# A four-layer graph network on one core: steps of the edge gathers, and the transposing loads, put at other pieces of a strip

## The chip, the cores and the metric

The kernel runs on one core of a Trainium2 chip. The metric is the device time of one execution in microseconds; the number compared is the median of several runs. The engines are named as in the profile: PE (matrix products), PEld (its weight loads), DVE (vector), ACT (scalar), POOL (GpSimd) and SP (sync, here a pure DMA issuer). A gather on POOL is an indirect DMA: POOL makes its descriptors, the DMA engines move the data afterwards.

## The reference, cut to what matters

6,250 nodes with 128 features pass through four pre-normalised graph layers over the same 206,250 edges, which are sorted by destination. All four need sums over edges; the first weights them:

```
msg = edge_val[:, None] * x[edge_src]
neighbor = jax.ops.segment_sum(msg, edge_dst, num_segments=N_NODES)
...
agg = jax.ops.segment_sum(x[src], dst, num_segments=n)          # layers 1 and 3
summed = jax.ops.segment_sum(gathered, node_idx, num_segments=n_nodes)   # layer 2: the other way round
```

Each is a product with a node-by-node matrix that holds how many edges (or what sum of weights) run between two nodes. The kernel builds that matrix once and uses it as a dense one.

## The kernel before, in words

**Two stages.** The first (here the *build*, from the start to about 1120 us in the trace) makes the matrix of counts and, on the way, layer 0. The second (`dense`, L890) multiplies by the stored counts for layers 1 to 3. The change touches the build alone.

**Strips and pieces.** The build walks 25 strips (`strip`, L825) of 256 destination nodes; the last has one block of 128, 106 of them real. A strip is cut into 32 counts of four windows each, and eight pieces, numbered 0 to 7, of four counts. For one count (`count`, L722) PE makes 24 pairs of weight load and product from two one-hot tiles, `s_hot` (source within its block of 128) and `k_hot` (number of the block, also times the three parts of the weight), into a PSUM tile `pK` of which there are three; then ACT copies it twice (L741): to `cnt` (counts) and `edge_w` (weights). DVE makes the one-hots of a piece a piece ahead (`one_hots`, L703, three instructions at L715, L717 and L718; two buffers each, so the ones for piece n+2 can start when PE is through with piece n). When half a strip is counted, that is after pieces 3 and 7, SP stores the block `cnt` to memory (L843, 1568 KB).

**What is threaded between the pieces.** After each piece the strip advances several generators by one step, in this order (L846 to L857):
- `end`: the end of layer 0 for the strip before last (`finish0`, L774), at pieces 0 to 5 and 7. Its step at piece 0 loads `xs0`, that at piece 4 stores two blocks (L799, L800), that at piece 7 one (L815).
- `edges`: the edges of the next strip (`prepare`, L628), at pieces 1, 3, 5 and 6. Its steps are: find by a comparison (L633 to L638) where the strip's edges start, and gather `line`; refine that (L643 to L663) and gather the first half of `dst`; count the matches (L669, L671), and gather the second half of `dst` and then `src` and the weights, each in two halves (five gathers, all issued by L625); after that turn them to keys (L676 to L688, DVE and POOL); transpose them on PE and copy them on ACT (L692, L697). The first of these steps, for the strip after next, is taken at piece 7.
- `before`: one eighth of layer 0's product for the strip before (`layer0`, L760): 12 or 14 products of `h0` and `edge_w`, at every piece.
- `turns` (`turn`, L743): one load that transposes seven blocks of counts (L751) and the store of the transposed load before it (L753), 175 of each in all, one at every piece from strip 1 on.

**What sets the order.** Strips 1 to 23 are under a manual schedule, so each engine runs its instructions in the order in which the program writes them; a step of a generator that waits holds up all that stands behind it on its engine. Strips 0 and 24 are ordered by the scheduler. POOL holds, in a strip: `line`, `dst`, `dst`, `src`, weights, `src`, weights, one addition of `finish0` (L798) and four instructions of `split` (L574 to L577). SP holds the stores of counts, the loads and stores of `turn` and those of `finish0`.

Of the kernel before, what the change touches and what calls it, by code (L numbers as in the profile page):

```python
# [469 lines left out]
NS = len(STRIPS)  # L470
# [16 lines left out]
def fast(ctx: ExitStack, tc: tile.TileContext, a: dict, out: bass.AP, flag: bass.AP):  # L487
# [84 lines left out]
    def split(eng, parts, src, rest):  # L572

        eng.tensor_copy(parts[0], src)  # L574
        eng.tensor_tensor(rest, src, parts[0], op=ALU.subtract)
        eng.tensor_copy(parts[1], rest)
        eng.tensor_tensor(parts[2], rest, parts[1], op=ALU.subtract)  # L577
# [7 lines left out]
    with ExitStack() as bx:  # L585
# [38 lines left out]
        def fetch(t, name, idx):  # L624
            nc.gpsimd.indirect_dma_start(out=t, out_offset=None, in_=col[name],  # L625
                                         in_offset=bass.IndirectOffsetOnAxis(ap=idx, axis=0))

        def prepare(k):  # L628

            n0 = node0[:, k : k + 1]  # L630
            junk = once.tile([P, NSMP], BF16, name="junk")
            r = small.tile([P, 1], F32, name="r")
            nc.vector.tensor_scalar(junk, smp, n0, None, op0=ALU.is_lt, op1=ALU.add, accum_out=r)  # L633
            at = small.tile([P, 1], F32, name="at")
            nc.vector.tensor_scalar(at, r, 1.0, 0.0, op0=ALU.subtract, op1=ALU.max)
            nc.vector.tensor_scalar(at, at, float(P), float(E - P), op0=ALU.mult, op1=ALU.min)
            at_i = small.tile([P, 1], I32, name="at_i")
            nc.vector.tensor_copy(at_i, at)  # L638
            line = once.tile([P, P], I32, name="line")
            fetch(line, "dst", at_i)  # L640
            yield
            less = once.tile([P, P], BF16, name="less")
            nc.vector.tensor_scalar(less, line, n0, None, op0=ALU.is_lt)  # L643
            c = small.tile([P, 1], F32, name="c")
            nc.vector.tensor_reduce(c, less, axis=mybir.AxisListType.X, op=ALU.add)
            off = small.tile([P, 1], F32, name="off")
            nc.vector.tensor_add(off, at, c)

            dst = once.tile([P, P], I32, name="dst")
            src = once.tile([P, P], I32, name="src")  # L650
            wgt = once.tile([P, P], F32, name="wgt")
            vals = pay.tile([P, 5, P], BF16, name="vals")
            same = once.tile([P, P], BF16, name="same")
            other = once.tile([P, P], BF16, name="other")
            halves_of = [(h, slice(h * H, (h + 1) * H)) for h in range(WN)]
            offs, nodes = [], []
            for h, half in halves_of:
                off_i = small.tile([P, 1], I32, name="off_i")
                nc.vector.tensor_scalar(off_i, off, float(E - H), None, op0=ALU.min)  # L659
                fetch(dst[:, half], "dst", off_i)  # L660
                offs.append(off_i)
                node = small.tile([P, 1], F32, name="node")
                nc.vector.tensor_scalar(node, n0, float(h), None, op0=ALU.add)  # L663
                nodes.append(node)
                if h + 1 == WN:
                    break
                yield
                here = deg[:, k, h : h + 1]
                nc.vector.tensor_scalar(same[:, half], dst[:, half], node, None, op0=ALU.is_equal,  # L669
                                        op1=ALU.add, accum_out=here)  # L670
                nc.vector.tensor_add(off, off, here)  # L671
            for (h, half), off_i in zip(halves_of, offs):
                fetch(src[:, half], "src", off_i)
                fetch(wgt[:, half], "edge_weight", off_i)
            yield
            nc.vector.tensor_scalar(same[:, half], dst[:, half], node, None, op0=ALU.is_equal,  # L676
                                    op1=ALU.add, accum_out=deg[:, k, WN - 1 : WN])
            for (h, half), node in zip(halves_of, nodes):
                nc.vector.tensor_scalar(other[:, half], dst[:, half], node, float(2 * P),
                                        op0=ALU.not_equal, op1=ALU.mult)  # L680
            sb = once.tile([P, P], I32, name="sb")
            nc.vector.tensor_scalar(sb, src, 7, None, op0=ALU.arith_shift_right)
            nc.vector.tensor_tensor(vals[:, 1, :], other, sb, op=ALU.add)
            sl = once.tile([P, P], I32, name="sl")
            nc.vector.tensor_scalar(sl, src, P - 1, None, op0=ALU.bitwise_and)
            nc.vector.tensor_copy(vals[:, 0, :], sl)
            rest = once.tile([P, P], F32, name="rest")
            split(nc.gpsimd, [vals[:, i, :] for i in (2, 3, 4)], wgt, rest)  # L688
            yield
            pv = psum.tile([P, 5, P], BF16, name="pD")  # L690
            for i in range(5):
                nc.tensor.transpose(pv[:, i, :], vals[:, i, :], identh)  # L692
            keys = pay.tile([P, P // TI, 2, TI], BF16, name="keys")
            parts = pay.tile([P, P // TI, 3, TI], BF16, name="by_edge")
            for t, i in ((keys, 0), (parts, 2)):
                to = pv[:, i : i + t.shape[2], :].rearrange("p i (q t) -> p q i t", t=TI)
                nc.scalar.copy(t, to)  # L697
            by_edge = keys, parts
            yield by_edge
# [3 lines left out]
        def one_hots(by_edge, t0):  # L703

            of = slice(t0 // TI, t0 // TI + tq)
            keys, parts = (t[:, of, :, None, :] for t in by_edge)

            def at(i, n):
                return keys[:, :, i].to_broadcast([P, tq, n, TI])

            def count_up(n):
                return iota[:, None, :n, :].to_broadcast([P, tq, n, TI])

            s_hot = hot.tile([P, tq, P, TI], BF16, name="s_hot")
            nc.vector.tensor_tensor(s_hot, count_up(P), at(0, P), op=ALU.is_equal)  # L715
            k_hot = hot.tile([P, tq, 4, NB, TI], BF16, name="k_hot")
            nc.vector.tensor_tensor(k_hot[:, :, 0], count_up(NB), at(1, NB), op=ALU.is_equal)  # L717
            nc.vector.tensor_tensor(k_hot[:, :, 1:], k_hot[:, :, :1].to_broadcast([P, tq, 3, NB, TI]),  # L718
                                    parts.to_broadcast([P, tq, 3, NB, TI]), op=ALU.mult)
            return s_hot, k_hot  # L720
# [101 lines left out]
        edges = prepare(1)  # L822
        next(edges)

        def strip(k, nb):  # L825
            nonlocal before, edges, by_edge, hots
            edge_w = edge.tile([P, NB, SW], F32, name="edge_w")
            end = ends.pop() if ends else iter(())
            last, piece, following = nb * P // WN, 0, None
            for w0 in range(0, last, PW):  # L830
                if w0 % TW == 0:
                    now, t1 = hots, w0 + TW
                    if t1 < last:
                        hots = one_hots(by_edge, t1)
                    elif following:
                        hots = one_hots(following, 0)
                if w0 * WN % P == 0:
                    cnt = cnts.tile([P, NB, P], BF16, name="cnt")
                count(w0, now, cnt, edge_w)
                g, w1 = k * SB + w0 * WN // P, w0 + PW  # L840
                if w1 * WN % P == 0:
                    c, i = CHUNK_OF[g]
                    nc.sync.dma_start(cnt_d[c, :, i, :], flat(cnt))  # L843
                if w1 % (PW * PT) and w1 < last:
                    continue
                if piece != 6:  # L846
                    next(end, None)
                if piece in (1, 3, 5):
                    next(edges, None)
                elif piece == 6:  # L850
                    following = next(edges, None)
                next(before, None)
                if piece == 7 and k + 2 < NS:
                    edges = prepare(k + 2)
                    next(edges)
                if k and piece < 8:
                    next(turns, None)  # L857
                piece += 1
            by_edge = following
            for _ in chain(before, end):  # L860
                pass
            before = layer0(k, nb, edge_w)
# [327 lines left out]
```

## Time and profile before

| | |
|---|---|
| median of 3 runs | 2080.66 us (2076.43 to 2086.75) |
| profiled execution | 2135.14 us |
| its span in the trace | 2133.1 us |
| mean granted clock of PE | 0.969 |
| busy over the span: PE, PEld, DVE, ACT, POOL | 1905.6, 1551.1, 1392.8, 1176.7, 403.6 us |
| ACT copies of `pK` (L741), two kinds, 784 of each | 404.5 and 413.1 us |
| gathers (L625), `dst` alone, 50 | 82.4 us, 1648 ns each |

Busy time counts when an engine has an instruction of its own in work. The share of the whole span says little here, since the build and the dense stage have different limits; what follows reads the build alone. "Idle before, and what ended it" names the last semaphore that came before an instruction could start; "remote" stands for a semaphore that rose at a moment where the profile has no instruction's end to go with it, "issue" for no wait that the profile shows.

### The profile page before, as it was taken

What the parts mean: (1) busy time and instruction counts of PE and PEld (TensorE: products, weight loads), DVE (VectorE), ACT (ScalarE), POOL (GpSimd) and SP (SyncE); (2) the same over time, 40 slices, a digit from 0 to 9 for tenths busy, and PEclk for the clock granted to TensorE, in tenths of its full rate; (3) what the DMA queues carried; (4) which work ended last, traced back from release to release, by engine and by line L of the source; (5) the groups of instructions that cost most, each with busy time, mean ns of one, the idle gap of its engine ahead of it and who ended that gap; (6) DMA issues with size and microseconds to landing.
All of it is one profiled execution on the core that took longest, in us unless ns stands there. A gap on an engine that the chain in (4) does not pass through costs nothing. (4 is left out here: it accounts for less than half of the span.)

```text
span 2133.1 us, 60004 instructions
## 1 busy us (share of the span) xinstructions
PE 1905.6 (89%) x25624; PEld 1551.1 (73%) x25624; DVE 1392.8 (65%) x2957; ACT 1176.7 (55%) x2717; POOL 403.6 (19%) x377
## 2 busy tenths in 40 slices
PE   1789999989989889999999589999698999999998
PEld 1677777777777777777778468888566777778775
DVE  5867777767777677777673577678775554443443
ACT  2855666666656566666563356566455554443443
POOL 3023222332222332223320110000411110000000
PEclk9999999999999999999999789999899999997999
DMA  2466777666776766766642998788576777866774
GB/s 59 121 168 163 168 186 183 159 177 172 187 175 156 187 163 161 194 171 176 161 113 102 267 291 274 222 275 274 156 221 180 225 237 240 257 193 201 238 235 131
DMA packets 423783, 406.29 MB, mean 190 GB/s; under 512 B 191216, under 2 KB 414307, under 8 KB 417235
## 3 DMA queue, kind: packets, MB, share of 16 engines
q1 hardware_dynamic: 414883, 394.35, 65.6%
q0 software_dynamic: 5600, 6.56, 1.2%
q8 instruction: 203, 3.33, 0.6%
q10 hardware_dynamic: 3024, 1.45, 0.4%
q14 instruction: 73, 0.60, 0.1%
HBM read 227.26 MB, written 134.89 MB: 170 GB/s over the span
## 5 line engine op out<-in xcount | busy, mean ns | idle before, releaser
L741 ACT CAST cnt<-pK 128x392 bf16<-128x392 f32 x784 | 404.5, 516 | 355.3 <-PE pK L736 261.7
L766 PE MATMUL pL<-edge_w,h 128*128 128x256 f32 (+1 forms) x2450 | 573.4, 385 | 3.7 <-issue 3.2
L736 PE MATMUL pK<-k_hot,s_hot 64*128 64x49 bf16 (+1 forms) x18816 | 418.9, 194 | 102.6 <-ACT edge_w L741 48.7
L736 PEld LDWEIGHTS <-s_hot 64*128 64x128 bf16 x18816 | 367.5, 96 | 193.9 <-issue 154.2
L766 PEld LDWEIGHTS pL<-edge_w,h 128*128 128x128 f32 x2450 | 452.8, 194 | 64.7 <-issue 6.1
L741 ACT COPY edge_w<-pK 128x392 f32<-128x392 f32 x784 | 413.1, 527 | 0.0
L922 PE MATMUL acc<-some,parts 128*128 128x512 f32 (+1 forms) x1456 | 373.8, 399 | 28.2 <-DVE some L917 20.5
L715 DVE TENSOR_TENSOR s_hot<-iota,keys 128x2048 bf16<-128x2048 bf16 x196 | 238.8, 1218 | 189.6 <-remote 127.8
L922 PEld LDWEIGHTS acc<-some,parts 128*128 128x128 f32 x1456 | 274.7, 197 | 91.3 <-DVE some L917 22.9
L911 ACT CAST others<-ring 128x1536 fp32r<-128x1536 bf16 (+3 forms) x156 | 192.4, 1233 | 203.3 <-PE acc L922 143.3
L718 DVE TENSOR_TENSOR k_hot<-k_hot,by_edge 128x2352 bf16<-128x2352 bf16 x196 | 283.7, 1447 | 8.0
L910 DVE CAST some<-ring 128x2048 fp32r<-128x2048 bf16 (+3 forms) x156 | 165.8, 1063 | 183.2 <-PE acc L922 169.8
L922 PE MATMUL acc<-others,parts 128*128 128x512 f32 (+1 forms) x1092 | 280.5, 392 | 0.0
L917 DVE TENSOR_SCALAR_CACHE_REDUCE some<-ring 128x512 fp32r<-128x512 bf16 (+1 forms) x364 | 216.5, 651 | 61.8 <-PE acc L922 34.0
L922 PEld LDWEIGHTS acc<-others,parts 128*128 128x128 f32 x1092 | 205.6, 195 | 42.2 <-issue 0.5
L920 ACT ACTIVATE others<-ring 128x512 fp32r<-128x512 bf16 (+1 forms) x273 | 162.3, 597 | 110.1 <-issue 53.5
L625 POOL DMA_INDIRECT dst<-in_dst,off_i x50 | 82.4, 1648 | 405.7 <-DVE off_i L659 222.6
L922 PE MATMUL acc<-some,q_parts 128*128 128x512 f32 (+1 forms) x390 | 112.7, 415 | 31.2 <-DVE some L910 31.2
L717 DVE TENSOR_TENSOR k_hot<-iota,keys 128x784 bf16<-128x784 bf16 x196 | 110.1, 562 | 0.0
L922 PEld LDWEIGHTS acc<-some,q_parts 128*128 128x128 f32 x390 | 71.9, 198 | 52.1 <-DVE some L910 36.1
L625 POOL DMA_INDIRECT line<-in_dst,at_i x25 | 40.6, 1626 | 291.1 <-DVE at_i L638 288.5
L922 PE MATMUL acc<-others,q_parts 128*128 128x512 f32 (+1 forms) x260 | 79.5, 415 | 0.0
(158 smaller groups left out, 1510.1 us busy)
## 6 DMA issues: line engine op xcount, KB each, us to landing
ring<-cnt_d SPq DMA_DIRECT2D x168, 896.0 KB
cnt_d<-cnt SPq DMA_DIRECT2D x49, 1568.0 KB
cntT_d<-tt SPq DMA_DIRECT2D x175, 224.0 KB
ring<-cntT_d SPq DMA_DIRECT2D x60, 640.0 KB
ring<-cnt_d SPq DMA_DIRECT2D x14, 224.0 KB
xs<-in_x SPq DMA_DIRECT2D x12, 256.0 KB
xs<-in_x SPq DMA_DIRECT2D x24, 128.0 KB
u_d<-xs SPq DMA_DIRECT2D x24, 128.0 KB
```

What stands on the lines that cost most here:

```text
L625: nc.gpsimd.indirect_dma_start(out=t, out_offset=None, in_=col[name], in_offset=bass.IndirectOffsetOnAxis(ap=idx, axis=0))
L715: nc.vector.tensor_tensor(s_hot, count_up(P), at(0, P), op=ALU.is_equal)
L717: nc.vector.tensor_tensor(k_hot[:, :, 0], count_up(NB), at(1, NB), op=ALU.is_equal)
L718: nc.vector.tensor_tensor(k_hot[:, :, 1:], k_hot[:, :, :1].to_broadcast([P, tq, 3, NB, TI]), parts.to_broadcast([P, tq, 3, NB, TI]), op=AL ...
L736: nc.tensor.matmul(pk[:, h, to], s_hot[r, u, :, t], rhs, start=j == 0, stop=True, skip_group_check=True)
L741: nc.scalar.copy(m.rearrange("p b (i h) -> p b i h", h=WN), by_block[:, i])
L766: nc.tensor.matmul(pl[:, :w], h0[:, s, :], edge_w[:, s, :w], start=s == 0, stop=s == NB - 1)
L910: nc.vector.tensor_copy(some[:, :dve, :nb], t[:, :dve])
L911: nc.scalar.copy(others[:, : step - dve, :nb], t[:, dve:])
L917: nc.vector.tensor_scalar(rhs, t[:, i], 1.0, None, op0=ALU.mult, op1=ALU.add, accum_out=total)
L920: nc.scalar.activation(rhs, t[:, i], AF.Copy, accum_out=total)
L922: nc.tensor.matmul(acc[:, :w], parts[:, q + i, j, :], rhs, start=q + i + j == 0, stop=q + i + j == last)
```

## The change

The generator of edges gets one more step: the `yield` after the four gathers of `src` and weights moves into their loop, so that the second `dst`, the first `src` and the first weights are issued at one step, the second `src` and weights at the next. The steps of the generators are then put at other pieces:

```diff
             for (h, half), off_i in zip(halves_of, offs):
                 fetch(src[:, half], "src", off_i)
                 fetch(wgt[:, half], "edge_weight", off_i)
-            yield
+                yield
...
+        END_AT, EDGES_AT, NEXT_AT = (0, 1, 2, 3, 4, 5, 7), (0, 2, 3, 5, 6), 6
+        TURN_AT = (1, 2, 2, 3, 5, 6, 6, 7)
...
-                if piece != 6:
+                if piece in END_AT:
                     next(end, None)
-                if piece in (1, 3, 5):
-                    next(edges, None)
-                elif piece == 6:
+                if piece in EDGES_AT:
                     following = next(edges, None)
                 next(before, None)
-                if piece == 7 and k + 2 < NS:
+                if piece == NEXT_AT and k + 2 < NS:
                     edges = prepare(k + 2)
                     next(edges)
-                if k and piece < 8:
+                for _ in range(TURN_AT.count(piece) if k else 0):
                     next(turns, None)
```

| step | piece before | piece after |
|---|---|---|
| find the start, gather `line` | 7 | 6 |
| refine, gather first half of `dst` | 1 | 0 |
| count matches, gather second half of `dst` | 3 | 2 |
| gather first halves of `src` and weights | 3 | 2 |
| gather second halves of `src` and weights | 3 | 3 |
| make keys | 5 | 5 |
| transpose and copy keys | 6 | 6 |
| turning loads (eight in a strip) | 0, 1, 2, 3, 4, 5, 6, 7 | 1, 2, 2, 3, 5, 6, 6, 7 |
| steps of `end` | 0 to 5, 7 | 0 to 5, 7 |

The number of instructions, their shapes and the buffers stay as they are.

## The prediction

> **What bounds the kernel now.** I read first the busy time of each engine over the build (from 200 to 1000 us PE is busy 92 us in 100, DVE 74, ACT 62, POOL 29), then one strip's pieces one by one, then the timeline of each engine in the piece that is too long, then the waits of the whole build. In this view each row is one piece of strip 9 (from PE's first product of a piece to that of the next): length, then busy time of PE, PEld, DVE, ACT, POOL, then granted clock, DMA share, GB/s.
>
> ```profile
> 449.45:454.73 5.28, 4.90 (x111) 4.17 (x110) 5.21 (x7) 3.58 (x9) 1.71 (x1) 1.00 1.06 311
> 454.73:460.48 5.75, 5.61 (x117) 4.88 (x117) 3.26 (x10) 3.21 (x8) 0.00 (x0) 1.00 0.93 201
> 460.48:465.35 4.87, 4.74 (x110) 4.01 (x110) 4.73 (x10) 3.31 (x9) 1.74 (x1) 1.00 0.34 93
> 465.35:470.20 4.85, 4.71 (x109) 3.98 (x109) 4.68 (x13) 3.21 (x8) 1.53 (x1) 1.00 0.17 71
> 470.20:477.20 7.00, 5.45 (x109) 4.18 (x109) 1.34 (x2) 2.58 (x7) 4.63 (x5) 1.00 0.91 272
> 477.20:483.07 5.87, 4.92 (x111) 4.19 (x110) 5.77 (x12) 4.94 (x13) 3.33 (x5) 1.00 0.45 73
> ```
>
> Pieces 2, 3 and 4 (rows 3 to 5) hold the same work for PE, 96 pairs and 12 products of layer 0, yet piece 4 takes 7.00 us and not 4.86. Piece 5 holds two transposes more and is 5.03 us where nothing disturbs it (strips 3 and 13), here 5.87. Pieces 2 and 3 are PE's own work end to end; pieces 4 and 5 are not. What happens there:
>
> ```profile
> 468.67 1.74 POOL L625 DMA_INDIRECT dst<-in_dst,off_i  x1 [5.24 <-DVE node L663]
> 470.71 1.59 POOL L625 DMA_INDIRECT src<-in_src,off_i  x1 [0.30 <-issue]
> 472.61 0.94 POOL L625 DMA_INDIRECT wgt<-in_edge_weight,off_i  x1 [0.30 <-issue]
> 473.86 0.94 POOL L625 DMA_INDIRECT src<-in_src,off_i  x1 [0.30 <-issue]
> 475.10 0.94 POOL L625 DMA_INDIRECT wgt<-in_edge_weight,off_i  x1 [0.30 <-issue]
> ```
> ```profile
> 472.25 0.49 PE L736 MATMUL pK<-k_hot,s_hot 64*128 64x98 bf16 x15 [0.48 <-ACT edge_w L741]
> 473.23 0.26 PE L736 MATMUL pK<-k_hot,s_hot 64*128 64x49 bf16 x4 [0.49 <-issue]
> 473.97 0.25 PE L736 MATMUL pK<-k_hot,s_hot 64*128 64x98 bf16 x5 [0.48 <-issue]
> ...
> 479.60 0.58 PE L736 MATMUL pK<-k_hot,s_hot 64*128 64x98 bf16 x24 [0.94 <-ACT edge_w L741]
> ```
> ```profile
> 477.14 1.23 DVE L715 TENSOR_TENSOR s_hot<-iota,keys 128x2048 bf16<-128x2048 bf16 x1 [5.66 <-remote]
> ```
> ```profile
> DVE s_hot L715 <- remote: 123.8, 22, 6.0
> ```
>
> The five gathers run from 468.67 to 476.04, beside the block of counts that SP stores from 468.82 (its packets: 469.3 to 474.3). PE's last products of piece 4 are on record by 474.22, but DVE, which waits for them, is let go at 477.14, 1.1 us after the last gather; ACT's last copy of the piece starts at the same 477.14. PE itself halts twice for half a microsecond with no wait on show, and in piece 5 it waits for ACT, which is late. The last line (waits, 60 to 1080 us) says that DVE's wait comes once in each of 22 strips. The release follows the end of the last gather by about 1 us in others too (strip 2: 0.9, strip 13: 1.0, strip 21: 0.9), so I take the word "remote" to mean: PE's completions arrive late while POOL issues gathers beside a busy store.
>
> The size: over strips 2 to 22 pieces 4 and 5 take 13.16 us together in the mean, against 4.87 + 5.03 = 9.90: 3.26 us too long, 68 us in 21 strips, some 75 with strips 1 and 23. That is the most the change can win there. A gather alone in a quiet piece (`dst` at 461.70, row 3) costs nothing: 4.87 against 4.85 us.
>
> **The change part by part.** *Turning loads.* Compared instruction by instruction, SP's order in the build is the same before and after: no other entry of SP lies between the slots the loads are moved across (behind the load of `xs0` at piece 0 came the loads of pieces 0, 1, 2, now those of 1, 2, 2; behind the stores of piece 4 came those of 4, 5, 6, now of 5, 6, 6). The loads at 3 and 7 still stand right behind the stores of counts. Nothing waits differently: 0 us, and no cover is needed.
>
> *Splitting five into three and two.* POOL's order is the same too. The last two gathers need only an address that DVE computed a step earlier, and wait for nothing of piece 3; POOL will run all five in one row, as before. By itself: 0 us.
>
> *What is left* is DVE's small work, and the gathers that hang on it, one piece earlier.
> - `line` (at 7, now 6): L633 to L638 is 1.88 + 0.09 + 3 x 0.15 us, with gaps 2.4 us, now in front of the one-hots at 442.76, where DVE stood idle 1.70 us for keys. They end 0.8 us later, near 446.7, and are used at 449.45: hidden, with 2.7 us to spare. The gather moves to about 443.9, out of the stretch of the other store.
> - First `dst` (at 1, now 0): five instructions, 1.1 us, put behind L781 at 452.7; DVE idled 2.2 us before 457.99. Hidden. The gather goes from 461.70 to about 454.1, among the turning loads (DMA share 0.93 in that row).
> - The five (at 3, now 2): 0.9 us of DVE in front of the one-hots at 464.4; those are for 470.2 and end at 467.6. Hidden, as long as the first `dst` lands by 466. Issued at 454.1 it has 12 us; at worst so far (`line` from 449.60, behind a store) data took to 454.5, 5 us.
>
> So the five begin at about 464.4 instead of 468.67. How long do they take? A gather takes 0.94 us with DVE idle, 1.59 to 1.74 beside one-hots, and DVE is busy without a break until about 470.7. The Trainium skill (SBUF — State Buffer, Who interferes with whom) says of a vector operation on two SBUF inputs that it contends with what GpSimd reads and not with what it writes, and infers that making descriptors needs only the write side. By that rule the row would be 5 x 0.94 + 4 x 0.30 = 5.9 us and over at 470.3, before much of the store. By the trace it is 1.74 + 1.60 + 1.70 + 0.94 + 0.94 + 4 x 0.30 = 8.1 us, over at 472.5. I take the trace: the third gather's tail and the last two still lie beside the store, against four before.
>
> If PE's completions come free 1.0 us after the last gather, that is 473.5 and not 477.1. Piece 4's last count is through PE at about 472.6, so ACT gets it 0.9 us late instead of 4.5, and piece 5 (475.1) finds its buffers free: the wait of 0.94 us there goes. PE's own halts (1.9 us in piece 4 at the median) were in the stretch from 472.3 on; I leave 0.7 us for what overlap remains. Saved: 2.9 (median excess) less 0.7 is 2.2 us, bounds 0 (the store alone does it) and 3.3. New costs: single gathers now run at the start of PE's pieces 7 and 1. The nearest row is `line` in piece 0 beside a store: 5.28 against 5.03 us for the like piece 5, 0.25 us at most; against it piece 0 gives that back. I take 0.3 us net, bounds 0 and 2. What is late next is nothing: pieces 4 and 5 become PE's own work like pieces 2 and 3.
>
> Sum: (2.2 - 0.3) x 22 strips = 42 us, from 2135.1 to about 2093 in a profiled execution. That one is 54.5 us above the median of the runs, and no view tells whether the pause is as long without recording; taking three quarters of it, 32 us, gives 2080.7 - 32 = 2049.
>
> **Rivals.**
> - *The change does not do what it says, and the shift does not matter either* (the pause belongs to the store and the turning load behind it, both unmoved): for it, three gathers still reach into the store, and POOL's and SP's orders are unchanged. Against: piece 0 has a store, a turning load and one gather and is only 0.25 us long. 2079.
> - *All of it goes*: the third gather starts at 468.5, before the store's packets, and two cause nothing. 75 us less in the trace; also PE's clock halves for 3.4 us eight times in the build, all of them in pieces 4 or 5. Gives 2080.7 - 72 = 2009.
> - *Slower: the first `dst` meets the turning loads.* It now runs at 454.1 to 455.8, where the DMA share is 0.93 and small packets are most of it, and in strips 12 to 16 PE already halts up to 1.1 us in piece 1 (6.2 to 6.7 us against 5.75). If completions are held there to 1 us after the gather, 456.8, count 1 of that piece (455.2) is 1.6 us late and the fourth, which needs its buffer, 1.2 us. With piece 4 unmended that is 22 x 1.2 = 26 us: 2107. It decides from where piece 1 loses more than pieces 4 and 5 win, 2.2 us; against it speaks `line` in piece 0.
>
> **How the numbers follow.** Most of the pause goes: 0.47, at 2049 (2025 to 2068 by its bounds). No effect: 0.25, 2079. All goes: 0.11, 2009. Slower: 0.17, 2107. About 0.5% (10 us) is what a measurement of this kernel can tell from no change. The first and third case are faster, less 0.01: 0.57; same 0.26; slower 0.17. The range from 2008 to 2092 takes in the first three and the mild part of the last.
>
> **What would show it.** In the changed trace the five gathers should start near piece 3's start, in one row with gaps of 0.30 us and 8 us long (5.9 would speak for the skill's rule). SP's order is as before. The wait of DVE's L715 for "remote" should fall from 5.6 us to below 3, pieces 4 and 5 to about 10.6 us together, and pieces 1 and 7 stay within 0.3 us of 5.75. I am wrong if piece 4 still ends in a release 1 us after a store's last packet (474.3) rather than after a gather, or if piece 1 takes over the pause.

## The result, and the profile after

Measured side by side on one chip, the changed kernel takes 2068.11 us (median of 14 runs, 2061.53 to 2077.33) against 2078.28 (14 runs, 2072.86 to 2086.75): ratio 0.9949, 95% interval 0.9935 to 0.9963. It is faster, by 10 us or 0.5%, where 32 us were forecast. Its profiled execution took 2067.12 us, span 2065.2, mean granted clock 0.967.

Against the profile of before, that span is 68 us shorter, nearly seven times the gain of the runs. The answer to the piece-by-piece view that was shown of before, strip 9, columns as there:

```profile
433.29:438.36 5.07, 4.89 (x111) 4.17 (x111) 2.85 (x8) 3.59 (x9) 0.82 (x1) 1.00 1.05 329
438.36:444.16 5.80, 5.60 (x117) 4.88 (x117) 4.18 (x12) 3.21 (x8) 0.92 (x1) 1.00 0.96 193
444.16:449.03 4.87, 4.74 (x110) 4.01 (x110) 4.77 (x11) 3.31 (x9) 0.94 (x1) 1.00 0.28 78
449.03:453.88 4.85, 4.71 (x109) 3.98 (x109) 4.74 (x7) 3.21 (x8) 3.94 (x4) 1.00 0.24 82
453.88:458.79 4.91, 4.73 (x110) 4.01 (x110) 2.99 (x4) 3.96 (x10) 2.40 (x3) 1.00 0.99 300
458.79:464.62 5.83, 4.96 (x112) 4.16 (x112) 4.39 (x12) 3.49 (x9) 3.58 (x5) 1.00 0.75 201
```

Piece 4 (fifth row) is 4.91 us where it was 7.00. Over strips 2 to 22, pieces 4 and 5 take 4.91 and 5.03 us at the median (before 6.75 and 6.08). POOL's timeline of the same strip:

```profile
448.09 1.74 POOL L625 DMA_INDIRECT dst<-in_dst,off_i  x1 [8.82 <-DVE node L663]
450.14 1.59 POOL L625 DMA_INDIRECT src<-in_src,off_i  x1 [0.30 <-issue]
452.04 1.21 POOL L625 DMA_INDIRECT wgt<-in_edge_weight,off_i  x1 [0.30 <-issue]
453.55 1.59 POOL L625 DMA_INDIRECT src<-in_src,off_i  x1 [0.30 <-issue]
455.45 0.94 POOL L625 DMA_INDIRECT wgt<-in_edge_weight,off_i  x1 [0.30 <-issue]
```

The five gathers begin a little before piece 3, in one row with gaps of 0.30 us, 8.3 us long. The forecast had every one of these signs. But the last two rows matter: they still run beside the block of counts that SP issues at 452.50, and piece 4 doesn't mind. Of the waits (60 to 1080 us), this is the row of DVE's L715 for PE:

```profile
DVE s_hot L715 <- PE pK L736: 50.6, 28, 2.1
```

"Remote", 123.8 us before, is gone from this engine. All this reads like a full success of the mechanism, at one and a half times the 42 us that were forecast between two profiled executions; the runs say 10 us. One of the two profiles is not of what the runs measured. Before's own time (2135.14) was 54.5 us above the median of its first three runs, and it is 48 us above the slowest of all 14; after's (2067.12) is one of its 14 runs and close to their median.

The kernel before takes 2078 and 2081 us on the chips of two comparisons (*calm* below) and 2123, 2127, 2127 and 2139 on those of four others (*pausing*), so each kernel is compared only with before on the same chip in the same comparison.

### The profile page after: what moved, and what is told of

The parts are those of the page before. It is cut to its first block, busy times and chain, and to the rows that moved or that the text cites. A ratio compares the mean times of both kernels' runs of the same rounds, so it can differ in the third digit from the quotient of the medians.

```text
span 2065.2 us, 60004 instructions
## 1 busy us (share of the span) xinstructions
PE 1869.4 (91%) x25624; PEld 1526.7 (74%) x25624; DVE 1395.9 (68%) x2957; ACT 1174.7 (57%) x2717; POOL 436.9 (21%) x377
## 5 line engine op out<-in xcount | busy, mean ns | idle before, releaser
L766 PE MATMUL pL<-edge_w,h 128*128 128x256 f32 (+1 forms) x2450 | 563.8, 381 | 0.9 <-issue 0.6
L766 PEld LDWEIGHTS pL<-edge_w,h 128*128 128x128 f32 x2450 | 446.5, 191 | 56.6 <-issue 1.0
L736 PEld LDWEIGHTS <-s_hot 64*128 64x128 bf16 x18816 | 361.3, 96 | 149.6 <-issue 125.3
L736 PE MATMUL pK<-k_hot,s_hot 64*128 64x49 bf16 (+1 forms) x18816 | 403.8, 194 | 66.0 <-ACT edge_w L741 25.8
L925 PE MATMUL acc<-some,parts 128*128 128x512 f32 (+1 forms) x1456 | 368.6, 394 | 35.0 <-DVE some L920 22.4
L925 PEld LDWEIGHTS acc<-some,parts 128*128 128x128 f32 x1456 | 268.7, 192 | 100.1 <-DVE some L920 27.7
L715 DVE TENSOR_TENSOR s_hot<-iota,keys 128x2048 bf16<-128x2048 bf16 x196 | 239.3, 1221 | 78.7 <-PE pK L736 50.6
L718 DVE TENSOR_TENSOR k_hot<-k_hot,by_edge 128x2352 bf16<-128x2352 bf16 x196 | 273.0, 1393 | 8.0
L925 PE MATMUL acc<-others,parts 128*128 128x512 f32 (+1 forms) x1092 | 275.1, 386 | 0.0
L925 PEld LDWEIGHTS acc<-others,parts 128*128 128x128 f32 x1092 | 200.7, 190 | 41.6 <-issue 0.5
L625 POOL DMA_INDIRECT src<-in_src,off_i x50 | 76.4, 1528 | 15.4 <-issue 14.9
```

The costliest lines, as they stand in the source:

```text
L736: nc.tensor.matmul(pk[:, h, to], s_hot[r, u, :, t], rhs, start=j == 0, stop=True, skip_group_check=True)
L766: nc.tensor.matmul(pl[:, :w], h0[:, s, :], edge_w[:, s, :w], start=s == 0, stop=s == NB - 1)
L925: nc.tensor.matmul(acc[:, :w], parts[:, q + i, j, :], rhs, start=q + i + j == 0, stop=q + i + j == last)
```

## The experiments

Two theories at first, for how 68 us in the profile become 10. *Unusual execution*: the profile of before shows a pause that most executions don't have. *Recording*: the pause is there only while a profile is taken. Beside them stood the open point of the forecast: is it gathers beside the store that make the pause? "Pieces" below are medians over strips 2 to 22 of one profile; ratios are to before in the same comparison, with their 95% interval behind them.

### Before again, and the two halves of the change

`b_again` is the kernel before, unchanged. `turns_only` is before with the turning loads moved, `gathers_only` the changed kernel with its loads at the old pieces, `five_at_2` before with its five gathers, unsplit, at piece 2 and nothing else:

```
turns_only    TURN_AT = (1, 2, 2, 3, 5, 6, 6, 7)    EDGES_AT, NEXT_AT = (1, 3, 5, 6), 7       (as before)
gathers_only  TURN_AT = (0, 1, 2, 3, 4, 5, 6, 7)    EDGES_AT, NEXT_AT = (0, 2, 3, 5, 6), 6    (as after)
five_at_2     TURN_AT = (0, 1, 2, 3, 4, 5, 6, 7)    EDGES_AT, NEXT_AT = (1, 2, 5, 6), 7
```

> The kernel before, unchanged, profiled once more. Theory A (the pause beside the store is real, but the execution recorded first had a far longer one than the usual): the profile comes near the timed runs, 2075 to 2090 us, and pieces 4 and 5 take about 10.4 us together in strips 2 to 22 instead of 13.2. Theory B (the pause is made by recording): the profile is again about 2135 us and pieces 4 and 5 about 13, while the timed runs stay at 2078. Ratio to the kernel before 1.000.

> The kernel before with the turning loads at 1, 2, 2, 3, 5, 6, 6, 7 and the edges untouched. Both theories: SP issues the same instructions in the same order, so 1.000 (0.998 to 1.002). If the slots of the loads carry the gain after all: 0.995.

> The changed kernel with the turning loads back at 0 to 7. Theory A and the reading of SP's order: the whole gain, 0.995. If the slots of the loads carry it: 1.000.

> The kernel before with one step moved: the second dst and the four gathers of src and weights at piece 2 instead of 3, unsplit; line stays at 7 and the first dst at 1, loads at 0 to 7. If the gain comes from moving the five off the store: 0.995 to 0.996. If it comes from the gathers of line and first dst: 1.000. Pieces 4 and 5 near 10.0 us in the profile under the first.

Measured, with before at 2126.53 us: `b_again` 2126.09 (0.9996, 0.9982 to 1.0010); `turns_only` 2127.21 (1.0003, 0.9984 to 1.0022); `gathers_only` 2120.38 (0.9979, 0.9966 to 0.9993); `five_at_2` 2117.05 (0.9968, 0.9946 to 0.9990). The profile of `b_again` (span 2127.7, pieces 4 and 5 at 6.67 and 5.97 us) agrees with its runs here. So it is neither an unusual execution nor something that separates the profiled execution from the others beside it: on this chip every run takes 48 us longer than in the first comparison. The moved loads alone are worth nothing, as forecast, and the moved gathers 4 to 7 us by their ratios. That is less than was expected of them, and the pause is still there: piece 4 takes 6.61 us in `gathers_only` and 7.03 in `five_at_2`, whose pieces 4 and 5 were to fall to 10.0 us together and take 12.1.

### Is it the gathers at all, and what else

The next comparison fell on a pausing chip too (before 2123.06): `b_third` is before, `after_again` the changed kernel. `no_gathers` is before, with the four gathers of `src` and weights only for the first strip; later strips keep its data, so the sources and weights of the others are left out. `turns_off_store` is before with the loads moved so that none stands between the store after piece 3 and those after piece 4 (the load behind the other store, after piece 7, moves too).

```diff
 no_gathers
-            for (h, half), off_i in zip(halves_of, offs):
+            for (h, half), off_i in zip(halves_of, offs) if k == 0 else ():
 turns_off_store
+        TURN_AT = (0, 1, 1, 2, 4, 5, 5, 6)
```

> The kernel before once more, for a profile from whichever chip this is. If it runs near 2078 us here, theory A (a pause that differs from chip to chip) expects pieces 4 and 5 at 10.0 to 10.6 us together in strips 2 to 22; if near 2126 us, about 12.9 as in the last look. If the profile shows 12.9 while the runs are near 2078, theory B (recording makes it).

> The changed kernel unchanged. On a chip where before takes 2078 us: 0.995. Where it takes 2126 us: 0.998, as the gathers alone gave there, with pieces 4 and 5 at about 12.1 us. If the turning loads' slots matter there: 0.994.

> The kernel before with the four gathers of src and weights issued for the first strip alone; the later strips use those values (left out: the other strips' sources and weights). If the gathers beside the store make the pause: pieces 4 and 5 fall to 9.9 to 10.3 us, and the ratio to 0.970 to 0.975 where before takes 2126 us, 0.994 to 0.996 where it takes 2078. If the store and the turning load make it by themselves: 0.998 to 1.000.

> The kernel before with the turning loads at 0, 1, 1, 2, 4, 5, 5, 6, so that none is issued between the store of counts after piece 3 and the stores of piece 4. If the pause needs only gathers and the store: 0.999 to 1.001. If the turning load behind the store is part of it: pieces 4 and 5 shorter by 1 us or more, 0.99 where before takes 2126 us.

Measured: `b_third` 2118.8 (one run); `after_again` 2117.99 (0.9973, 0.9954 to 0.9991); `no_gathers` 2062.81 (0.9715, 0.9692 to 0.9737); `turns_off_store` 2092.97 (0.9865, 0.9843 to 0.9886). Pieces 4 and 5 of `no_gathers`, strip 9, columns as in the view of pieces:

```profile
449.26:454.17 4.91, 4.73 (x109) 4.00 (x109) 3.95 (x4) 3.97 (x10) 0.40 (x2) 1.00 1.00 303
454.17:460.02 5.85, 4.95 (x111) 4.16 (x110) 4.88 (x12) 3.49 (x9) 2.42 (x5) 1.00 0.71 192
```

The store is there (303 GB/s in the first row), the gathers are not (POOL 0.40 us), piece 4 is 4.91, and DVE has no wait for "remote": on a pausing chip the store without the gathers makes no pause, and leaving them out takes 60 us away. The loads kept away from the stores take 30, in piece 4 (5.34 us; piece 0, beside the other store, stays at 5.26). And `after_again` shows where the change's gain stays on such a chip: its pieces 0 to 7 are 5.07, 6.19, 4.87, 5.17, 6.53, 5.03, 5.11 and 5.74 us, against 5.27, 5.75, 4.87, 4.85, 6.66 and 6.06 of `b_third` for the first six. Piece 5 gives 1.0 us, piece 4 keeps its pause, and pieces 1 (0.44) and 3 (0.32) lengthen. Its waits (60 to 1080 us) tell what stayed:

```profile
DVE s_hot L715 <- remote: 43.4, 20, 2.2
PE pK L736 <- issue: 40.3, 83, 1.8
```

In `b_third` these are 117.4 and 27.4 us. DVE is let go much sooner, about 2.5 us before the end of the row's last gather and not 1 us after it; but PE's own halts, for which the profile shows no wait, grew.

### Is it the store beside them

If a row of gathers beside the store makes the pause, moving either out of the other's way must end it. Four kernels, before at 2139.08 us: `gathers_and_turns_off` is the changed kernel with the loads of `turns_off_store`; `five_at_1` has the five gathers, unsplit, at piece 1 and the loads at 0 to 7; `five_at_1_turns_off` the same with those other loads; `store_late` the changed kernel with loads at 0 to 7 and each block of counts stored one piece later.

```diff
 five_at_1
+        EDGES_AT, NEXT_AT = (0, 1, 5, 6), 6
 store_late
-                    nc.sync.dma_start(cnt_d[c, :, i, :], flat(cnt))
+                    waiting.append((cnt_d[c, :, i, :], flat(cnt)))
...
+                if piece in (0, 4) and waiting:
+                    nc.sync.dma_start(*waiting.pop(0))
```

> The changed kernel with the turning loads at 0, 1, 1, 2, 4, 5, 5, 6, so that none is issued between the store after piece 3 and the stores of piece 4. If gather, store and turning load have to meet, and the two edits add: 0.983 to 0.987 where before takes 2123 us (0.9865 for the loads alone, 0.997 for the gathers alone). If they take the same time away: 0.986.

> The changed kernel with the five gathers unsplit at piece 1 instead of 2 and 3, loads at 0 to 7: they run from about 461 to 469, over before the packets of the store. If a gather must lie beside the store to make the pause: piece 4 at 4.9 us, 0.972 to 0.980 where before takes 2123 us. If gathers beside turning loads cause as much: pieces 2 and 3 lengthen by as much as piece 4 gives back, 0.995 to 1.000.

> The kernel of the run before, and no turning load behind the store after piece 3 (loads at 0, 1, 1, 2, 4, 5, 5, 6). If the pause is gathers beside the store: 0.972 to 0.978, little below the run before. If the store and the load each matter by themselves: lower by another 0.01.

> The changed kernel with each store of counts issued one piece later (after pieces 4 and 0), loads at 0 to 7: the gathers, which end near 472.5 in strip 9's times, and the store, from 475, no longer meet. If a gather beside the store makes the pause: pieces 4 and 5 near 10.0 us, 0.975 to 0.980 where before takes 2123 us. If the load beside gathers is enough: piece 4 stays over 6 us and the ratio over 0.99.

Measured: 2126.37 (0.9944, 0.9924 to 0.9963); 2159.81 (1.0088, 1.0055 to 1.0121); 2140.88 (1.0006, 0.9983 to 1.0029); 2125.84 (0.9954, 0.9932 to 0.9975). The three that separate gathers and store, `five_at_1`, its variant and `store_late`, missed what the theory expected. So did `gathers_and_turns_off`: the loads' new places, worth 30 us in `turns_off_store`, add little where the gathers stand a piece earlier (0.9944 against 0.9973 of `after_again`, on another chip). In `store_late`, strip 9, pieces 3 and 4, then POOL, then SP:

```profile
464.66:469.89 5.23, 4.81 (x109) 3.99 (x110) 2.19 (x5) 2.63 (x7) 4.29 (x4) 1.00 0.38 98
469.89:476.53 6.64, 5.29 (x110) 4.15 (x110) 5.63 (x6) 4.74 (x12) 1.86 (x2) 1.00 0.05 12
```
```profile
463.73 1.74 POOL L625 DMA_INDIRECT dst<-in_dst,off_i  x1 [9.21 <-DVE node L663]
...
470.17 1.67 POOL L625 DMA_INDIRECT wgt<-in_edge_weight,off_i  x1 [0.30 <-issue]
```
```profile
464.12 0.52 SPq L753 DMA_DIRECT2D cntT_d<-tt  x1
477.58 0.37 SPq L799 DMA_DIRECT2D u_d<-xs  x1
```

SP issues nothing from 464.6 to 477.58, the DMA engines are idle (share 0.05 in the second row), and still piece 4 takes 6.64 us. In `five_at_1_turns_off` the row of gathers runs from 467.73 to 475.65, and the pause is in piece 3, where none was before:

```profile
471.70:479.18 7.48, 5.44 (x111) 4.19 (x110) 4.73 (x7) 3.41 (x8) 3.35 (x3) 1.00 0.22 73
```

So the theory of the forecast falls: the pause goes with the row of gathers wherever that is put, store or no store. In `five_at_1` piece 3 is longer still (8.94 us at the median against 7.45), but not from loads beside the row: in strip 9 the row runs from 475.69 to 483.61, and SP issues nothing from 474.72 to 485.51, and most strips are alike. What differs is PE's granted clock, 0.69 over that piece:

```profile
479.65:489.82 10.17, 8.19 (x109) 5.96 (x108) 5.18 (x7) 3.41 (x8) 3.35 (x3) 0.69 0.45 153
```

PE's 12 products of layer 0 take 5.49 us in it and not 2.86. The clock is at half for 65 us of strips 2 to 22 in `five_at_1`, for 20 in `five_at_1_turns_off`, 27 in `b_third` and 0 in `turns_off_store` and on a calm chip. Half the clock can cost at most half of that time. So the clock may cost `five_at_1` up to 22 us more than its variant, and these strips differ by 21; of the 30 us of `turns_off_store` up to 14 may be the clock's. Its DVE still waits 88.7 us for "remote" (117.4 in `b_third`), so the gathers are felt there too. Why the clock drops more often in some of these kernels stays open.

### Both kernels on a calm chip

What was then still missing was a profile of before on a chip like that of the first comparison. The next comparison had one (before 2080.86 us). `b_fourth` is before, `after_third` the changed kernel. `gated` gives every gather of `src` and weights a step and a DVE-written address of its own, so that none follows another in a row; `gated_turns_off` also takes the loads of `turns_off_store`.

```diff
+            yield
             for (h, half), off_i in zip(halves_of, offs):
-                fetch(src[:, half], "src", off_i)
-                fetch(wgt[:, half], "edge_weight", off_i)
-                yield
+                for t, name in ((src, "src"), (wgt, "edge_weight")):
+                    gate = small.tile([P, 1], I32, name="gate")
+                    nc.vector.tensor_copy(gate, off_i)
+                    fetch(t[:, half], name, gate)
+                    yield
...
+        EDGES_AT, NEXT_AT = (0, 1, 2, 3, 4, 5, 6, 7), 6
+        TURN_AT = (0, 1, 2, 3, 4, 5, 6, 7)          # gated_turns_off: (0, 1, 1, 2, 4, 5, 5, 6)
```

> The kernel before once more, to see its pieces on whatever chip this is. If the chip is of the kind on which it took 2078 us, its pieces 4 and 5 should take about 10 us together and not 12.9, and what is left against the changed kernel shows where 10 us came from; if it takes 2120 to 2140 again, they take 12.7 to 13.2.

> The changed kernel once more beside it. On a chip of the first kind: pieces as in its first profile, 41.5 us a strip. On one of the second kind: 43.7 us, piece 4 at 6.5, and 5 to 9 us below the kernel before.

> The changed kernel with every gather of src and weights at a step of its own (dst at 7 and 0, then 1, 2, 3, 4), each with an address that DVE copies at that step, so that POOL cannot run them in a row; turning loads at 0 to 7. If it is the row of five that makes the pause, it goes: 0.972 to 0.980. If every gather costs the same wherever it stands, it stays, spread over the pieces: 0.995 to 1.000. If single gathers beside loads cost more: over 1.002.

> The same with the turning loads at 0, 1, 1, 2, 4, 5, 5, 6. If row of gathers and load behind a store are two causes that add up, it is the fastest so far: 0.970 to 0.976. If the load matters only beside a row of gathers, the same as gated within 0.002. If gathers cost the same everywhere, 0.985 to 0.995.

Measured: `b_fourth` 2087.98 and `after_third` 2074.23 (one run each); `gated` 2071.36 (0.9949, 0.9930 to 0.9968); `gated_turns_off` 2062.15 (0.9906, 0.9877 to 0.9936). The first two came as expected; the large gains that were thought possible for the last two needed a pause, and there was none to take away. Pieces 4, 5 and 6 of strip 15, of `b_fourth` and then of `after_third`:

```profile
710.82:715.81 4.99, 4.74 (x109) 4.00 (x108) 4.00 (x4) 3.96 (x10) 4.08 (x4) 1.00 1.01 321
715.81:720.84 5.03, 4.89 (x111) 4.16 (x111) 2.70 (x10) 3.49 (x9) 3.77 (x5) 1.00 0.39 117
720.84:726.65 5.81, 5.15 (x114) 4.25 (x114) 4.29 (x5) 3.87 (x10) 2.80 (x3) 1.00 0.65 167
```
```profile
708.12:713.03 4.91, 4.73 (x111) 4.00 (x110) 2.99 (x4) 3.97 (x10) 2.38 (x3) 1.00 0.98 305
713.03:718.06 5.03, 4.89 (x113) 4.16 (x112) 3.86 (x11) 3.49 (x9) 3.15 (x4) 1.00 0.72 199
718.06:723.17 5.11, 4.98 (x116) 4.25 (x116) 4.97 (x8) 3.87 (x10) 1.15 (x2) 1.00 0.91 168
```

The first row settles it: here before has its store under way (321 GB/s), gathers beside it (POOL busy for 4.08 of 4.99 us), and no pause. Nor has its list of waits any DVE row for "remote". Medians of pieces 4 and 5 over strips 2 to 22 are 4.96 and 5.03 us, and the granted clock is 1.00 there. What differs is the third row, piece 6. In the mean of those strips it is 5.56 us against 5.11; all other pieces differ by 0.05 us or less, and 0.48 us a strip x 21 is 10 us, the gain of the runs. Piece 6 holds the five transposes of keys (L692). PE's timeline there in `b_fourth`, then POOL's:

```profile
722.92 0.40 PE L692 MATMUL pD<-f_identh,vals 128*128 128x128 bf16 x4
723.84 0.23 PE L692 MATMUL pD<-f_identh,vals 128*128 128x128 bf16 x1 [0.53 <-POOL vals L577]
```
```profile
709.36 1.74 POOL L625 DMA_INDIRECT dst<-in_dst,off_i  x1 [4.61 <-DVE node L663]
...
717.38 0.94 POOL L625 DMA_INDIRECT wgt<-in_edge_weight,off_i  x1 [0.30 <-issue]
718.34 0.74 POOL L798 TENSOR_TENSOR xs<-xs,h 128x256 f32<-128x256 f32 x1
719.94 0.36 POOL L574 CAST vals<-wgt 128x128 bf16<-128x128 f32 x1 [0.86 <-DMA wgt<-in_edge_weight,off_i]
...
722.31 1.47 POOL L577 TENSOR_TENSOR vals<-rest,vals 128x128 bf16<-128x128 f32 x1
```

And POOL's in `after_third`:

```profile
702.32 1.74 POOL L625 DMA_INDIRECT dst<-in_dst,off_i  x1 [8.71 <-DVE node L663]
...
709.68 0.94 POOL L625 DMA_INDIRECT wgt<-in_edge_weight,off_i  x1 [0.31 <-issue]
...
715.90 0.29 POOL L574 CAST vals<-wgt 128x128 bf16<-128x128 f32 x1 [1.73 <-DMA wgt<-in_edge_weight,off_i]
...
718.14 0.63 POOL L577 TENSOR_TENSOR vals<-rest,vals 128x128 bf16<-128x128 f32 x1
```

Read upwards: PE can't transpose the last part of the weights before POOL's `split` has made it at 723.78, while PE has stood ready since its fourth transpose. `split` waits for weights whose gather was issued at 717.38, 3.5 us before piece 6 begins, and then takes 3.84 us; in the changed kernel the last gather is out 8.4 us ahead of the piece, the split is over at 718.77, and PE never waits. The waits of `b_fourth` (470 to 1060 us) show the size, and those of `after_third` have no row of L692:

```profile
DVE sb L682 <- DMA src<-in_src,off_i: 28.1, 14, 2.4
...
PEld L692 <- POOL vals L577: 6.9, 13, 0.7
PE pD L692 <- POOL vals L577: 4.9, 13, 0.6
```

The wait comes in strips 10 to 22 alone: piece 6 takes 5.83 us there in the mean, 13 times 0.72 us too much, or 9.4 us. In strips 2 to 9 of the same trace piece 5 takes 5.86 to 6.40 us and not 5.03 (in the changed kernel too), the split is over in time, and piece 6 takes 5.11 to 5.15: a piece that is late hides the wait of the next.

`gated`, with its loads at the old pieces and its gathers apart, has piece 6 at 5.11 us too and the very ratio of the change, 0.9949. So on a calm chip the gain needs neither the moved loads nor the row, and there is no pause that gathers kept apart could take away. It also shows how little was missing: in strip 15 its last gather is out 3.8 us before piece 6, its split takes 2.44 us, and PE does not wait. `gated_turns_off` gains 9 us more (the two intervals overlap by 0.0006): piece 5 goes from 5.37 to 5.04 us in the mean (in strips 2 to 9) and piece 1 from 6.05 to 5.94, and PE's waits before its pairs for nothing that the profile names ("issue") fall from 15.1 to 7.0 us (60 to 1060 us).

### One more try at the gathers' place

`five_at_3` puts the five gathers of the changed kernel back to piece 3 and keeps its other moves; `five_at_2_again` is `five_at_2`.

```diff
-        EDGES_AT = (0, 2, 3, 5, 6)
+        EDGES_AT = (0, 3, 3, 5, 6)
...
-                if piece in EDGES_AT:
+                for _ in range(EDGES_AT.count(piece)):
                     following = next(edges, None)
```

> The changed kernel with its five gathers back at piece 3; the search for the strip's start, the first gather of dst and the loads stay where the change puts them. If the 10 us come from the gathers alone (src and weights land in time, so that PE no longer waits 0.5 us for the last key before its fifth transpose in piece 6), they are gone: 0.999 to 1.001, piece 6 at 5.6 to 5.7 on a chip without the pause. If the other moves bring them: 0.994 to 0.996, piece 6 at 5.11. On a chip with the pause PE is late in piece 5 anyway and piece 6 shows nothing.

> The kernel before with nothing but its five gathers, unsplit, at piece 2 instead of 3. On a chip without the pause: if the gathers alone bring the 10 us, 0.994 to 0.996 with piece 6 at 5.11; if not, 0.999 to 1.001.

The chip was a pausing one (before 2127.2), where piece 6 hides nothing and shows nothing (5.11 in both). `five_at_3` took 2155.47 (1.0133, 1.0101 to 1.0165), with piece 4 at 8.88 us; `five_at_2_again` 2121.38 (0.9944, 0.9914 to 0.9973). The question of the calm chip wasn't answered. What came out is that on a pausing chip the gathers' place is worth more within the changed schedule (1.0133 against about 0.997) than on its own. The clock has part in it: it is at half for 61 us of strips 2 to 22 in `five_at_3`, and for 24 to 27 in the three profiles of before that show the pause.

## Why the prediction was half right and half wrong

**The pieces and the order** were read rightly. The order of SP, the row of five, its start at piece 3, its 8.3 us (8.1 by the rows of before; 5.9 by the estimate from the Trainium skill, SBUF — State Buffer, Who interferes with whom) and the worthless move of loads (`turns_only` 1.0003, on a pausing chip) came as written.

**The step that failed first is the last one of the sum**: "taking three quarters of it, 32 us, gives 2080.7 - 32". The pause was measured in an execution of 2135 us and carried over to runs of 2081, with the words that no view tells whether it is as long there. On a chip like that of the comparison it is not there at all: `b_fourth` has 4.96 and 5.03 us in pieces 4 and 5, so this term, put at 32 us, was nothing. Of the two numbers at hand, a pause of 68 to 75 us and an excess of 54.5 us of that execution over the median, the second was to be subtracted from the first, not a quarter taken off: 68 - 54.5 leaves about 14 us of this pause to be won. That the 10 measured lie near this is no proof of it: they came from elsewhere (below).

**The cause of the pause** was the second error: "PE's completions arrive late while POOL issues gathers beside a busy store". The gathers half is shown on a pausing chip (`no_gathers`, 0.9715), the store half is refuted (`store_late`, `five_at_1_turns_off`). Hence the same move is worth only 5.7 us where the pause exists (`after_again`), not 42. The assumption that completions come free 1.0 us after the last gather did not hold for the changed kernel: DVE got its release before the end of the row, as shown, and still piece 4 stayed long, because PE's own halts stayed. The term "I leave 0.7 us for what overlap remains" measured 1.7 (6.53 against 4.86). In the means of strips 2 to 22, pieces 4 and 5 give 0.74 us and piece 0 gives 0.18, while pieces 1 and 3 take 0.32 each: 0.28 us a strip, 6 us in 21. The new cost, 0.3 us net for single gathers, measured 0.44 in piece 1 less 0.20 in piece 0 on pausing chips (medians), near enough, and 0.01 on the calm one (means; 0.12 by the medians of piece 1).

**What was won was not in the sum.** "What is late next is nothing" was asked of the work after the gathers' pause, not of the work that needs their data. On the calm chip that is the transposes of piece 6, 0.45 us a strip. In the profile of before they had no wait, because the pause made PE late by more than that, as piece 5 does in strips 2 to 9 of `b_fourth`: the pause hid the very wait that the runs contained.

**The rivals.** "No effect" (2079) is 11 us off the other way, "all goes" (2009) and "slower" (2107) are out. The slower rival's mechanism, a first `dst` among the turning loads, is there on pausing chips at 0.44 us in piece 1, a third of its price.

**Open.** Why some chips pause under a row of gathers and others don't, and whether it is the chip at all: each was met in one comparison only, and which chip the first comparison and the profile of before had is not on record. Whether each gather or only a row of them does it (`gated` ran on a calm chip alone), and whether it is POOL's work or the data moved. How the 10 us divide between the five gathers and the earlier `line` and first `dst`: the trace puts 0.45 of 0.48 us a strip at the wait for the gathers' data, but the runs meant to divide them met a pausing chip. And why `five_at_3` is 28 us slower than before: at most 19 of them are the clock's by the figures above.

## What to carry to other kernels

Compare a profiled execution's own time with the median of the runs before anything is costed from it: what it has in excess is not in the runs, and must come off the stall first. A stall also hides the waits behind it, so ask of every moved transfer who needs its data next and how much slack that one would have without the stall. A change whose gain rests on a stall of unknown cause should be weighed by the experiment that takes the suspected cause away altogether. And before two lengths of a stall are compared, look at the granted clock of both.

## What the runs showed of the hardware

The same kernel takes 2078 to 2081 us in two comparisons and 2123 to 2139 in four others, and on a pausing chip the time goes with gathers on POOL: with four of the row of five left out, it needs 2062.81 us, less than a calm one for the whole kernel. On a pausing chip PE halts in the piece in which a row of gathers ends (6.6 us for 4.9, with the DMA share at 0.05), and in `store_late` DVE is let go at 469.79, 2.6 us after the product it waits for ends by the profile, which models such ends. PE's granted clock falls to half only on pausing chips in strips 2 to 22, mostly in such a piece (10.17 us at 0.69 in `five_at_1`); on a calm chip it is 1.00. There that piece takes 4.96 us with the same row beside the store, against 4.91 with the row a piece earlier. Loads kept away from the block stores brought 30 us on a pausing chip (`turns_off_store`), at most 14 of them by the clock, little with the gathers a piece earlier (`gathers_and_turns_off`), and 9 on a calm one (`gated_turns_off` against `gated`). The fastest kernel seen on a calm chip is `gated_turns_off`, 0.9906 of before.
